# Gated experts with residual in fp32: carried pair sums closed from their PSUM banks, the second pass's x operands made during the first pass, and the last two pairs of features multiplied straight into rows

## The chip, the cores and the metric

The kernel runs on one core of a Trainium2 chip. The metric is the device time of one execution in microseconds (us). The engines are named as in the profile: PE (TensorE, with PEld for its weight loads), DVE (VectorE), ACT (ScalarE), POOL (GpSimd) and SP (SyncE, which issues nearly all DMAs here).

## The reference, cut to what matters

```python
# x: (8, 512, 256); 8 experts and one shared expert; F = 1024
g = einsum('bsd,edf->ebsf', x, Wg);  u = einsum('bsd,edf->ebsf', x, Wu)
expert_outs = einsum('ebsf,efd->ebsd', silu(g) * u, Wd)
expert_output = einsum('be,ebsd->bsd', gates, expert_outs)
shared = (silu(x @ Sg) * (x @ Su)) @ Sd
return x + (1 - sg) * expert_output + sg * shared
```

Everything is fp32. Each of the nine experts is evaluated for every token.

## The kernel before

The eight sequences are done in two passes `h` of four (NI = 4), so that a pass needs the transposed x of four sequences only. A pass goes over nine experts and two groups of four 128-wide pieces of F: 18 units in a pass, 36 in all, numbered `u.n` = 0 to 35. In one unit, four pieces `i` of the weights meet four sequences `j`, so there are 16 feature tiles h[i, j] of 128 x 512. Gate and up (`m` = 0 and 1) contract over D = 256, two halves of 128.

Plainly this would be 64 matmuls of 128 x 512 for gate and up and 32 for down. The kernel spends 52 and 26. It gives the weight pieces and sequences constants CI = (0, 1, -1, 2) and treats the six pairs in PAIRS, (1,0), (0,2), (3,0), (1,2), (3,1), (3,2), together: differences and sums of operands are prepared so that part of the products is shared.

**Gate and up** (`gate_up`). A unit has 52 steps "G". The first 16 are the hub, on the diagonal tiles: `P_step` (L370), `Q_step` (L392) and, for pair 0, `R1_step`. Then come six blocks, one for each pair, of two `R1_step` (L411) for the pair after it and four `R_step` (L421). The chain of one tile is: ACT copies a start value into a PSUM bank (L406, `seed`), PE adds a matmul (L411), DVE makes the start of the partner bank from it (L416), PE adds L421, DVE adds a kept tile where needed (L426), ACT takes silu of the gate bank (L356), and DVE multiplies gate, coefficient and up bank into h (L361). The banks `g0` and `g1` have three buffers each. DVE also makes the difference X of a pair's two features (L435). POOL adds the features up into four `rows` and four `cols` sums (L446), and prepares the weight forms (L291 to L313, L340, L345). `make_ad` (ACT, L333) makes `a2`, twice the first half of the down weights, which the forms of some pairs use.

**Down** (`down`) runs up to a unit behind, in steps "D" between the G steps, from G number 22 of its own unit to G 22 of the next. The two banks `po0` and `po1` alternate. A pair takes three matmuls: r = Wd h[i,j] (L494), S = Wd h[j,i] (L483), and a second one on top of r's bank with X (L511). Sums are carried over all 18 units of a pass in SBUF: B_j, b_j (the two halves of the output), V_p and S_p. `put` adds a bank to such a sum on DVE (L470). `carried` does it on PE: ACT copies the sum into the bank (L482), the matmul adds, ACT copies the bank out (L487). In the kernel before all six S_p are carried this way (OWN = all pairs). Then, for each i, one matmul of `rows` into b_i ("p", L483) and one of `cols` into B_i ("q", L494).

**Closing a pass.** In the last unit of each pass (u.n = 17 and 35) the sums are combined. `pair` appends to a list `combos`: V -= S, B_i -= S, b_i += V/d, b_j -= V/d; `ends_of` appends B_i -= c b_i. `combine` takes entries from the list and runs each as a DVE operation with both operands in SBUF (L557, L559). Then `turn_back` transposes every 128 x 128 block on PE (L143, `pto`), adds x (L584) and stores.

**x operands of the second pass.** In unit 17, from G 18, `turn_x` loads rows of x, transposes them on PE (`ptx`) and evicts them (L165, L169); `make_forms` makes the pair forms v, b0, b1 for pairs 0 to 2 (DVE L185 to L188, POOL L189), and unit 18 makes the other three (L205, L207, L219, L220). Forms are stored to DRAM (`xs`); each unit loads them from there (L209 for v, L226 for b).

The order on PE and POOL is the order of the program text (`manual_schedule`, HAND; in unit 0 ACT's too). The order on DVE, ACT and SP is set by a scheduler when the kernel is built. `ORDER` is the string of G and D steps of a unit: `HUB = "GGD" * 8`, then six times `"GGDGGDGGD"`.

Of the kernel before, what the change touches and what calls it, by code (L numbers as in the profile page):

```python
# [16 lines left out]
def kernel(  # L17
# [37 lines left out]
    nc = tc.nc  # L55
# [11 lines left out]
    OWN = (0, 1, 2, 3, 4, 5)  # L67
# [17 lines left out]
    iopool = ctx.enter_context(tc.tile_pool(name="io", bufs=2))  # L85
# [37 lines left out]
    made = []  # L123
    xhub = {}

# [29 lines left out]
    def turn_x(h, pool, tag, loaded=None):  # L155

        rows = loaded or [load_rows(pool, tag, NI * h)]
        for i in range(NI):
            xt = xpool.tile([P, 2, S], F32, tag="x", name=f"x{h}_{i}")
            for n_, k in enumerate((0, 1) if CI[i] == 0.0 else (1, 0)):  # L160
                pt, n = new_po(f"ptx{h}_{i}_{k}", h > 0)
                turn(pt, [rows[i][t // 2][:, t % 2, ts(k, P)] for t in range(NT)])
                turned[n] = True
                if k == 1:
                    nc.scalar.copy(xt[:, 1], pt)  # L165
                elif CI[i] == 0.0:
                    ve.tensor_copy(xt[:, 0], pt)
                else:
                    ve.scalar_tensor_tensor(  # L169
                        xt[:, 0], xt[:, 1], -CI[i], pt, ALU.mult, ALU.add  # L170
                    )
                if n_ == 1:
                    xhub[h, i] = xt
                    if len(rows) < NI:
                        rows.append(load_rows(pool, tag, NI * h + i + 1))
                yield

    def make_forms(h, p):

        i, j = PAIRS[p]  # L180
        d = CI[i] - CI[j]
        v, b0, b1 = (
            zpool.tile([P, S], F32, tag="z", name=f"f{k}{h}_{p}") for k in range(3)
        )
        ve.tensor_sub(v, xhub[h, i][:, 0], xhub[h, j][:, 0])  # L185
        if d != 1.0:
            ve.tensor_scalar(v, v, 1.0 / d, None, ALU.mult)
        ve.tensor_add(b0, v, xhub[h, j][:, 1])  # L188
        gp.tensor_tensor(b1, v, xhub[h, i][:, 1], ALU.add)  # L189
        made.append((h, p, (v, b0, b1)))  # L190

    def store_made():
        for h, p, tiles in made:
            scratch[h, p] = dram.tile([P, 3, S], F32, tag=f"xs{h}_{p}", name=f"xs{h}_{p}")
            for k, t in enumerate(tiles):
                nc.sync.dma_start(scratch[h, p][:, k], t)
        made.clear()
# [126 lines left out]
    def make_ad(u):  # L324
        a, A = u.raw_d[:, :, 0:P], u.raw_d[:, :, P : 2 * P]
        t = dpool.tile([P, NI - 1, P], F32, tag="ad", name=f"ad{u.name}")
        for i in range(NI):
            u.ad[i] = A[:, i]
            if CI[i] != 0.0:
                u.ad[i] = t[:, i - 1]  # L330
                at_of(u.ad[i], CI[i], a[:, i], A[:, i])
        u.a2 = dpool.tile([P, NI, P], F32, tag="a2", name=f"a2{u.name}", bufs=1)
        nc.scalar.mul(u.a2, a, 2.0)  # L333
# [96 lines left out]
    def h_sums(u, p):  # L430


        i, j = PAIRS[p]
        u.X[p] = tpool.tile([P, S], F32, tag="t", name=f"X{p}_{u.name}")
        ve.tensor_sub(u.X[p], u.h_[j, i], u.h_[i, j])  # L435
        for k, l in ((i, j), (j, i)):
            for which, n in (("rows", k), ("cols", l)):
                u.sums.append((which, n, (k, l)))
# [13 lines left out]
    combos = []  # L452

    def down(u, acc):
# [21 lines left out]
        def carried(key, w, b):  # L476

            po, k = new_po(f"{key[0]}{key[1]}_{u.name}")
            seeded = key in acc and not turned[k]
            turned[k] = False  # L480
            if seeded:
                nc.scalar.copy(po, acc[key])  # L482
            nc.tensor.matmul(  # L483
                po, w, b, start=not seeded, stop=True, skip_group_check=seeded
            )
            if seeded:
                nc.scalar.copy(acc[key], po)  # L487
            else:
                put(key, po, 1.0)

# [6 lines left out]
        def pair(p):  # L497
            i, j = PAIRS[p]
            d = CI[i] - CI[j]
            A, k = single(("r", p), u.Wd[p][i], u.h_[i, j])  # L500
            put(("B", j), A, 1.0)
            held[k] = True
            yield
            if p in OWN:
                carried(("S", p), u.Wd[p][j], u.h_[j, i])
            else:
                o, _ = single(("s", p), u.Wd[p][j], u.h_[j, i])
                put(("B", i), o, -1.0)
                put(("V", p), o, -1.0)
            yield  # L510
            nc.tensor.matmul(  # L511
                A, u.Ud[p], u.X[p], start=False, stop=True, skip_group_check=True
            )
            put(("V", p), A, 1.0)
            held[k] = False
            po_next[0] = 1 - k
            if u.closes:
                V, b = acc["V", p], (acc["b", i], acc["b", j])
                if p in OWN:
                    combos.append((V, -1.0, acc["S", p]))  # L520
                    combos.append((acc["B", i], -1.0, acc["S", p]))
                combos.append((b[0], 1.0 / d, V))
                combos.append((b[1], -1.0 / d, V))
            yield

        def ends_of(i):
            if CI[i] != 0.0:
                combos.append((acc["B", i], -CI[i], acc["b", i]))
            combos.append((u.h, i, acc))

        for p in range(5):
            yield from pair(p)
        for what in ("p0", "q0", 5, "q1", "p1", "q2", "p2", "q3", "p3"):
            if what == 5:
                yield from pair(5)
                continue
            i = int(what[1])
            if what[0] == "p":
                flush_sums(u, "rows", i)
                carried(("b", i), u.raw_d[:, i, 0:P], u.rows[i])  # L540
# [4 lines left out]
            if u.closes and what in ("q0", "p1", "p2", "p3"):  # L545
                ends_of(i)
            yield

    def combine():

        to, s, what = combos.pop(0)
        if not isinstance(s, float):
            h, i, acc = to, s, what
            for r in (0, 1):
                ends[h, i, r] = acc["bB"[r], i]
        elif s in (1.0, -1.0):
            ve.tensor_tensor(to, to, what, ALU.add if s > 0 else ALU.subtract)  # L557
        else:
            ve.scalar_tensor_tensor(to, what, s, to, ALU.mult, ALU.add)  # L559
# [13 lines left out]
    def turn_back(h, i, r):  # L573

        b = NI * h + i
        block = ends.pop((h, i, r))
        xr = load_back(h, i, r)
        if h + 1 < NH:
            pt, n = new_po(f"pto{b}_{r}", True)
            turned[n] = True  # L580
        else:
            pt = ps_g.tile([P, S], F32, tag=f"g{r}", name=f"pto{b}_{r}")
        turn(pt, [block[:, ts(t, P)] for t in range(NT)])
        ve.tensor_add(xr, pt.rearrange("p (t d) -> p t d", t=NT), xr)  # L584
        nc.sync.dma_start(block_of(out, b, r), xr)
        n = BACK.index((i, r)) + 1
        if h + 1 < NH and n < len(BACK):
            load_back(h, *BACK[n])

# [5 lines left out]
    def gate_up(u, nxt):  # L595
# [41 lines left out]
        for p in range(len(PAIRS)):  # L637
# [9 lines left out]
            if p == 5:  # L647
                store_made()
                if nxt is not None:
                    load_d(nxt)  # L650
# [19 lines left out]
    FIRST = "TGGTGGTGG" + "G" * 16 + BLOCK * 5  # L670

# [17 lines left out]
    turning = turn_x(0, hpool, "h", loaded)  # L689
# [8 lines left out]
    behind, acc = iter(()), {}  # L698
    for u in units:
# [6 lines left out]
        for what in ORDER if u.n else FIRST:  # L706
            if what == "G":
# [6 lines left out]
                if final and nxt is not None:  # L714
                    if nG == 18:
                        turning = turn_x(u.h + 1, iopool, "io")
                    if nG >= 18 and nG % 3 == 0:
                        next(turning, None)
                    if nG in (33, 39, 45):
                        make_forms(u.h + 1, (nG - 33) // 6)  # L720
                    if nG in (39, 45, 51):
                        store_made()
                if nG > TAKE and nG % 2 == 0 and len(u.sums) > 0:
                    add_sum(u)
# [4 lines left out]
            elif what == "T":  # L729
                for _ in range(2):  # L730
                    next(turning, None)
            else:
                next(behind, None)
                since_close += 1
                for _ in range(2 if nxt is not None else len(combos)):
                    if combos:
                        combine()
                if since_close in BACK_AT:
                    turn_back(u.h - 1, *BACK[BACK_AT.index(since_close)])
        for _ in g:  # L740
            pass
        if u.n == 0:
# [4 lines left out]
    for n, at in enumerate(BACK):  # L747
        load_back(NH - 1, *at, *((zpool, "z") if n < 6 else (iopool, "io")))
    for _ in behind:
        while combos:  # L750
            combine()
    for i, r in ((0, 0), (0, 1), (1, 0), (1, 1), (2, 0), (2, 1), (3, 0), (3, 1)):
        turn_back(NH - 1, i, r)
# [37 lines left out]
```

## Time and profile before

| | us |
|---|---|
| median of three runs | 2517.24 |
| lowest, highest | 2516.68, 2518.9 |
| the profiled execution, whole time | 2516.66 |
| its span, first to last instruction | 2514.8 |
| PE busy in the span | 2454.0 (98%) |
| POOL busy | 2080.4 (83%) |
| DVE busy | 1891.1 (75%) |
| ACT busy | 1328.8 (53%) |
| mean granted PE clock | 0.994 |

A matmul of 128 x 512 in fp32 is two instructions in the profile, so counts on PE are twice those in the code. Times in the trace are microseconds from the start of the span. An "idle before" of an engine is the time it stood still before an instruction, with what ended it. Durations in a list overlap a little[...]; so the distance between two starts is the better measure of what one costs.

### The profile page before, as it was taken

The numbers are of one execution on the slowest core, as the hardware profiler recorded it, in microseconds if no ns is written. First come the engines' busy times: TensorE is split into PE (matmuls) and PEld (weight loads), VectorE is DVE, ScalarE is ACT, GpSimd is POOL, SyncE is SP. The second block draws the span as 40 slices with busy tenths as digits, with TensorE's granted clock in tenths as the row PEclk, the third lists the DMA queues.
The fourth block names the chain that finished last, engine by engine and source line by source line (L and its number), as shares of the span: only waits on it lengthen the run. The fifth ranks groups of instructions, "written<-read, shape, count | busy, mean of one in ns | idle before, by whom it ended". The sixth has DMA issues, their size and how long they took to land.

```text
span 2514.8 us, 22640 instructions
## 1 busy us (share of the span) xinstructions
PE 2454.0 (98%) x5752; PEld 1079.7 (43%) x5752; DVE 1891.1 (75%) x2758; ACT 1328.8 (53%) x2484; POOL 2080.4 (83%) x2296
## 2 busy tenths in 40 slices
PE   7999999999999999999799999999999999999996
PEld 3444444444444444444344444444444444444442
DVE  6677777777777777777987777777777777777778
ACT  4555555555555555555345555555555555555552
POOL 6888888888888888888688888888888888888884
PEclk9999999999999999999999999999999999999999
DMA  4332333333333223333443333323333333333231
GB/s 147 96 90 84 91 100 97 100 101 101 93 100 92 91 87 94 89 96 93 142 135 99 93 89 96 93 87 89 96 96 101 101 100 98 95 94 95 84 96 42
DMA packets 180464, 242.97 MB, mean 97 GB/s; under 512 B 13296, under 2 KB 121840, under 8 KB 180336
## 3 DMA queue, kind: packets, MB, share of 16 engines
q1 hardware_dynamic: 180048, 241.49, 31.7%
q8 instruction: 48, 0.79, 0.1%
q14 instruction: 80, 0.66, 0.1%
q10 hardware_dynamic: 288, 0.04, 0.0%
HBM read 227.84 MB, written 13.63 MB: 96 GB/s over the span
## 4 chain that ended last, share of the span: by engine, by line
PE 93%; DVE 4%; issue 1%; ACT 1%; DMA 0%; POOL 0%; DVEq 0%; SPq 0%; ACTq 0%; POOLq 0%
PE c L421 28%; PE c L411 14%; PE c L392 10%; PE c L370 10%; PE r L511 7%; PE S L483 7%; PE r L494 7%; PE b L483 5%; PE q L494 5%; DVE h L361 1%; DVE accV L557 1%; DVE X L435 0%; DVE c L426 0%; DVE accB L557 0%; DVE accb L557 0%
## 5 line engine op out<-in xcount | busy, mean ns | idle before, releaser
L421 PE MATMUL c<-b,wb 128*128 128x512 f32 x1728 | 851.0, 594 | 0.0
L361 DVE SCALAR_TENSOR_TENSOR h<-sg,coef,c 128x512 f32<-128x512 f32 x576 | 428.5, 744 | 359.7 <-PE c L421 248.0
L356 ACT ACTIVATE sg<-c 128x512 f32<-128x512 f32 x576 | 344.5, 598 | 619.2 <-DVE c L426 360.4
L421 PEld LDWEIGHTS c<-b,wb 128*128 128x128 f32 x1728 | 328.2, 191 | 407.9 <-issue 385.2
L411 PE MATMUL c<-v,u 128*128 128x512 f32 x864 | 445.0, 597 | 16.4 <-ACT c L406 11.5
L446 POOL TENSOR_TENSOR rows<-rows,h 128x512 f32<-128x512 f32 x288 | 383.8, 1333 | 3.8 <-DVE h L361 3.8
L446 POOL TENSOR_TENSOR cols<-cols,h 128x512 f32<-128x512 f32 x288 | 369.6, 1283 | 0.0
L416 DVE TENSOR_TENSOR c<-D,c 128x512 f32<-128x512 f32 x432 | 299.4, 693 | 91.0 <-ACT sg L356 69.6
L312 POOL TENSOR_TENSOR wb<-u,wb 128x256 f32<-128x256 f32 x108 | 80.9, 749 | 295.4 <-ACT wb L310 295.4
L426 DVE TENSOR_TENSOR c<-c,D 128x512 f32<-128x512 f32 x432 | 299.2, 693 | 22.8 <-PE c L421 21.3
L370 PE MATMUL c<-x,w 128*128 128x512 f32 x576 | 276.7, 593 | 2.5 <-ACT sg L356 1.8
L411 PEld LDWEIGHTS c<-v,u 128*128 128x128 f32 x864 | 161.2, 190 | 233.7 <-issue 182.1
L511 PE MATMUL r<-X,ud 128*128 128x512 f32 x432 | 224.0, 600 | 11.2 <-DVE accB L470 11.2
L483 PE MATMUL S<-h,wd 128*128 128x512 f32 x432 | 222.1, 596 | 6.5 <-ACT S L482 6.4
L494 PE MATMUL r<-h,wd 128*128 128x512 f32 x432 | 221.5, 594 | 0.0
L435 DVE TENSOR_TENSOR X<-h,h 128x512 f32<-128x512 f32 x216 | 212.8, 985 | 5.9
L392 PE MATMUL c<-x,at 128*128 128x512 f32 x432 | 210.2, 595 | 1.2 <-DVE P L385 1.1
L446 POOL TENSOR_TENSOR rows<-h,h 128x512 f32<-128x512 f32 x144 | 207.2, 1439 | 0.0
L398 ACT COPY D<-c 128x512 f32<-128x512 f32 x288 | 169.1, 588 | 58.2 <-DVE h L361 58.1
L482 ACT COPY S<-accS 128x512 f32<-128x512 f32 x201 | 119.0, 592 | 140.1 <-DVE accV L470 132.1
L446 POOL TENSOR_TENSOR cols<-h,h 128x512 f32<-128x512 f32 x144 | 186.7, 1296 | 0.0
L375 ACT COPY P<-c 128x512 f32<-128x512 f32 x216 | 126.6, 587 | 101.9 <-PE c L370 97.2
(90 smaller groups left out, 3318.4 us busy)
## 6 DMA issues: line engine op xcount, KB each, us to landing
b<-xs SPq DMA_DIRECT2D x207, 512.0 KB, 3.5
v<-xs SPq DMA_DIRECT2D x207, 256.0 KB, 2.6
w<-in_L_cond_Wg_dram SPq DMA_DIRECT2D x128, 128.0 KB, 3.4
w<-in_L_cond_Wu_dram SPq DMA_DIRECT2D x128, 128.0 KB, 3.6
wd<-in_L_cond_Wd_dram SPq DMA_DIRECT2D x32, 512.0 KB, 4.9
xs<-b SPq DMA_DIRECT2D x9, 512.0 KB, 3.1
xin<-in_x_dram SPq DMA_DIRECT2D x16, 256.0 KB, 3.9
xr<-in_x_dram SPq DMA_DIRECT2D x16, 256.0 KB, 3.1
```

The lines of the kernel that those rows point to most:

```text
L356: nc.scalar.activation(s, bank, AF.Silu)
L361: ve.scalar_tensor_tensor(t, u.sg[i, j], coef[:, u.e, b : b + 1], bank, ALU.mult, ALU.mult)
L370: nc.tensor.matmul(bank, u.raw[i][:, m, 0], xhub[u.h, i][:, 0], start=True, stop=True)
L392: nc.tensor.matmul(bank, u.at[i][:, m], xhub[u.h, i][:, 1], start=False, stop=True, skip_group_check=True,)
L411: nc.tensor.matmul(bank, u.U[p][:, m], u.V[p], start=False, stop=True, skip_group_check=True)
L416: ve.tensor_sub(other, u.Ds[j, m], bank)
L421: nc.tensor.matmul(bank, u.W[p][:, r, m], u.VB[p][:, r], start=False, stop=True, skip_group_check=True,)
L426: ve.tensor_add(bank, bank, u.Ds[j, m])
L446: gp.tensor_tensor(sums[n], u.h_[n, n] if first else sums[n], u.h_[at], ALU.add)
L483: nc.tensor.matmul(po, w, b, start=not seeded, stop=True, skip_group_check=seeded)
L494: nc.tensor.matmul(po, w, b, start=True, stop=True)
L511: nc.tensor.matmul(A, u.Ud[p], u.X[p], start=False, stop=True, skip_group_check=True)
```

## The change

1. **Closing from the banks.** `combos`, `combine` and `ends_of` are gone. In the closing units S goes from its bank into B_i and V (two `put`); DVE adds the carried V into the bank of r in place, and the bank is put into b_i and b_j. What `carried` returns (the bank, where it was seeded) is put into B_i in place of the SBUF sum.
2. **OWN = (0, 1, 2, 3)**: S of pairs 4 and 5 is not carried; in every unit it is put from its bank into B_i and V.
3. **`a2`** is made by POOL in place of ACT.
4. **`prepare`** makes the x operands of the second pass in units 2 to 13, one step at every fourth D step: loads, transposes, evictions to the `io` pool (4 buffers, before 2), stores to DRAM, then for each of the six pairs four loads, three or four POOL operations and three stores. Unit 17 loads the finished x (`load_x`).
5. **The last unit** has its own order, LAST. Pairs 4 and 5 are not "starred" there: no X, no sums, no down matmuls of their own; their carried sums are closed in unit 34. Their four features h[1,3], h[3,1], h[3,2], h[2,3] are multiplied as stationary operands with the down weights (`tail`: four matmuls of 256 columns each), straight into rows of the output. x for the end is loaded as rows (two tiles of 2 KB a partition for each sequence), and stored so. The down steps of this unit are closer together, and transposes, tails and stores (B, X, S) are interleaved with the last G steps.

```diff
-    OWN = (0, 1, 2, 3, 4, 5)
+    OWN = (0, 1, 2, 3)
...
+    def prepare(h):
...
+        for i in range(NI):
+            to = xdram[h, i] = dram.tile([P, 2, S], F32, tag=f"xd{h}_{i}", name=f"xd{h}_{i}")
+            rows = load_rows(iopool, "io", NI * h + i)
...
+            for k in (1, 0):
+                pt, n = new_po(f"ptx{h}_{i}_{k}", True)
+                turned[n] = True
+                turn(pt, [rows[t // 2][:, t % 2, ts(k, P)] for t in range(NT)])
+                both[k] = tile_of(f"xt{i}_{k}_")
+                if k == 1 or CI[i] == 0.0:
+                    nc.scalar.copy(both[k], pt)
+                else:
+                    ve.scalar_tensor_tensor(both[0], both[1], -CI[i], pt, ALU.mult, ALU.add)
+                yield
...
+        for p, (i, j) in enumerate(PAIRS):
...
+            v = at[0]
+            gp.tensor_tensor(v, v, at[1], ALU.subtract)
+            if d != 1.0:
+                gp.tensor_scalar(v, v, 1.0 / d, 0.0, ALU.mult, ALU.add)
+            yield
+            gp.tensor_tensor(at[2], v, at[2], ALU.add)
+            yield
+            gp.tensor_tensor(at[3], v, at[3], ALU.add)
...
+            for k, n in ((0, 0), (1, 2), (2, 3)):
+                nc.sync.dma_start(to[:, k], at[n])
...
-        nc.scalar.mul(u.a2, a, 2.0)
+        gp.tensor_scalar(u.a2, a, 2.0, 0.0, ALU.mult, ALU.add)
...
+    def starred(u, p):
+        return u.n + 1 < len(units) or p < 4
+    def closes(u, p):
+        return u.closes and starred(u, p) or u.n + 2 == len(units) and p >= 4
...
-            if p in OWN:
-                carried(("S", p), u.Wd[p][j], u.h_[j, i])
+            args = u.Wd[p][j], u.h_[j, i]
+            if p in OWN and not closes(u, p):
+                carried(("S", p), *args)
             else:
-                o, _ = single(("s", p), u.Wd[p][j], u.h_[j, i])
+                if p in OWN:
+                    o, full = seeded(("S", p), *args)
+                    if not full:
+                        ve.tensor_add(o, o, acc["S", p])
+                else:
+                    o, _ = single(("s", p), *args)
                 put(("B", i), o, -1.0)
                 put(("V", p), o, -1.0)
...
-            put(("V", p), A, 1.0)
+            if closes(u, p):
+                ve.tensor_add(A, A, acc["V", p])
+                put(("b", i), A, 1.0 / d)
+                put(("b", j), A, -1.0 / d)
+            else:
+                put(("V", p), A, 1.0)
...
+        if u.n + 1 < len(units):
+            order = (0, 1, 2, 3, 4, "p0", "q0", 5, "q1", "p1", "q2", "p2", "q3", "p3")
+        else:
+            order = (0, 1, 2, "q0", 3, "p0", "q3", "q1", "p3", "q2", "p1", "p2")
...
+    def tail(u, i, j, first):
+        for t in range(NT):
+            bank = tails[j][t // 2][:, t % 2]
+            nc.tensor.matmul(
+                bank, u.h_[i, j][:, ts(t, P)], u.raw_d[:, i],
+                start=first and t % 2 == 0, stop=True, skip_group_check=True,
+            )
...
+    LAST = (
+        HUB + BLOCK * 4 + "GDGDGDGDGGD" + "GDGDBGDBGDGDGDS"
+        + "BBXBBXBBXXSSS"
+    )
...
-                if final and nxt is not None:
-                    if nG == 18:
-                        turning = turn_x(u.h + 1, iopool, "io")
...
+                if final and nxt is not None and nG in (18, 21, 24, 27):
+                    load_x(u.h + 1, (nG - 18) // 3)
...
+                if ahead is not None and u.n >= 2 and since_close % 4 == 0:
+                    next(ahead, None)
```

## The prediction

> **What bounds the kernel now.** I read the engines' busy time by stretches first, since shares over the whole span hide the ends (columns: window, its length, then busy us and instruction count of PE, PEld, DVE, ACT, POOL; granted clock; DMA):
>
> ```profile
> 0.00:85.00 85.00, 70.79 (x174) 30.32 (x175) 52.95 (x76) 37.76 (x70) 62.17 (x82) 0.96 0.43 143
> 85.00:1165.00 1080.00, 1079.09 (x2511) 475.48 (x2510) 804.79 (x1187) 591.46 (x1109) 913.62 (x1015) 1.00 0.31 94
> 1165.00:1325.00 160.00, 142.08 (x358) 62.98 (x357) 142.44 (x193) 68.38 (x126) 124.74 (x123) 0.96 0.40 127
> 1325.00:2440.00 1115.00, 1112.74 (x2589) 490.19 (x2588) 827.19 (x1222) 611.98 (x1146) 942.25 (x1050) 1.00 0.31 94
> 2440.00:2515.00 75.00, 49.34 (x126) 20.73 (x124) 63.76 (x81) 19.27 (x36) 37.65 (x29) 0.93 0.19 58
> ```
>
> In the two long stretches PE is full: 1080 / 2511 = 0.43 us an instruction, 0.86 a matmul. At this pace the others lose: the start has 134 full instructions and 32 transposes of 0.11 us (61 of 85 us used: 24 lost), the middle 294 and 64 (133 of 160: 27 lost), the end 94 and 32 (44 of 75: 31 lost). Some 80 us are to be had, none in between.
>
> Next, the list by line says what DVE costs (mean ns last):
>
> ```profile
> L470 DVE TENSOR_TENSOR accV<-r,accV 128x512 f32<-128x512 f32 x204 | 139.4, 683 | 0.8 <-PE r L511 0.4
> L557 DVE TENSOR_TENSOR accV<-accV,accS 128x512 f32<-128x512 f32 x12 | 16.1, 1344 | 0.0
> ```
>
> The timeline of DVE and then of PE in the last unit (start, us, operation, idle before it) shows the closing operations in a row, and PE waiting behind them:
>
> ```profile
> 2461.90 1.39 DVE L435 TENSOR_TENSOR X<-h,h 128x512 f32<-128x512 f32 x1
> 2463.22 1.75 DVE L557 TENSOR_TENSOR accV<-accV,accS 128x512 f32<-128x512 f32 x1
> 2464.89 1.75 DVE L557 TENSOR_TENSOR accB<-accB,accS 128x512 f32<-128x512 f32 x1
> 2466.56 3.42 DVE L559 SCALAR_TENSOR_TENSOR accb<-accV,accb 128x512 f32<-128x512 f32 x2
> ```
> ```profile
> 2471.24 1.12 PE L511 MATMUL r<-X,ud 128*128 128x512 f32 x2 [2.83 <-DVE accB L470]
> 2481.77 1.12 PE L511 MATMUL r<-X,ud 128*128 128x512 f32 x2 [3.37 <-DVE accB L470]
> 2491.97 2.07 PE L483 MATMUL S<-h,wd 128*128 128x512 f32 x2 [5.76 <-ACT S L482]
> ```
>
> DVE is 97% busy from 2436 to 2491 (53.15 of 55 us) and from 1191 to 1255 (61.78 of 64): it is the bound of both closings. At the start POOL and ACT hold each other up over a2:
>
> ```profile
> 33.46 0.73 POOL L345 TENSOR_TENSOR wd<-ud,a 128x256 f32<-128x256 f32 x1 [3.49 <-ACT a L333]
> ```
> ```profile
> 37.86 0.63 ACT L333 ACTIVATE a<-wd 128x512 f32<-128x512 f32 x1 [3.54 <-POOL wd L345]
> ```
>
> [...] 683 ns from a bank, 1344 from two SBUF tiles beside a busy POOL. [...] the matmul at 2491.97, behind a 5.76 us wait, took 2.07 us, others 1.02.
>
> **The change, part by part.** The base is the profiled execution: span 2514.8, 2516.66 in all, 0.6 below the median.
>
> *Start, a2.* POOL now makes a2 itself. Not in the trace; [...] 1.33 (two inputs here); I take 0.9. POOL then goes on at about 30.9 where it went on at 33.46: 2.6 earlier. ACT's seeds at 33.21 lose the 0.53 of a2 ahead of them, and its silu at 38.40 no longer queues behind the second a2. The next limit is L421 at 34.88 and the DVE/ACT chain after it, so PE's 42.09 moves by 2 to 3. I take -2.5 (bounds 0 and -5).
>
> *Steady units, DVE.* S of pairs 4 and 5: two puts each, 4 x 0.60 us a unit (starts back to back are 0.60 apart); ACT drops four copies of 0.59. Cover: in the hub after 686 DVE idles 1.95, 1.59, 0.57, 1.61 us, waiting for PE or ACT. S of pair 4 (L483 at 687.60) ends at 688.6, inside the 1.95; S of pair 5 (700.48) at 701.5, inside the 1.61. I cost it at 0; without that cover it is 2.4 us a unit.
>
> *Steady units, POOL.* a2 sits at the head of the hub, where POOL ran from 683 to 649 of the next cycle without a pause. Behind it queue the last sums; the tightest is the cols sum that ended at 641.24 for the q matmul at 643.43: 2.2 us of slack, against 0.9. Cost 0. After the hub POOL idles 3.04, 3.54, 2.04 us on ACT wb, so it recovers.
>
> *Units 2 to 13, prepare.* POOL: 6 x 3 additions and three scalings, 18 x 1.3 + 3 x 0.9 = 26 us over some 7.5 units; where two meet a2 in a hub, 0.9 + 2.6 passes the 2.2. SP: 8 row loads, 8 + 18 stores and 24 loads, in one queue with v, b and the weights. A store waits for POOL or ACT, a load for a store that frees its buffer, about 3 us (xs<-b lands in 3.1); a b load has 7.7 - 3.5 = 4.2 us to spare. So mostly hidden: I take +3 (0 to 15). The 8 transposes (0.44 us each, 3.5) move here from unit 17; one follows an S matmul on the same bank and waits for its eviction: +1 beyond the 3.5.
>
> *Middle.* Before, each closing pair took DVE 14 us (its L416 starts at 1203.33, 1217.31, 1231.80), where PE needs 9 x 0.86 = 7.7. Now a pair has 13 operations: ten at 0.60, two h at 0.65, one X at 1.0: 8.3 us. One loop comes in: the last b put frees the bank, ACT seeds it (0.6), PE runs S (1.0), DVE takes S; DVE has 1.8 us of other work for it, so I add 0.3: 8.6. Five pairs from about 1191.9 (1.3 earlier, since three transposes are gone): 9.4 + 3 x 8.6 + 7.5 + some waiting ends at 1235.5, before 1253.7: -18.2. Hub and turn-back after it, with fewer queued DVE operations: 18.5 to 17.0 us and 2.5 of PE waits and clock: -4. The 3.5 of transposes come back above: -19 net (bounds -13, -23).
>
> *Unit 34.* Pairs 4 and 5 close there: four more DVE operations on top of the four, 2.4 us more in a hub whose 5.9 us of idle they share: +0.7 (0 to 2).
>
> *End.* PE: 12 instructions of 0.43 less, 32 of half length more: +1.7 us, inside what follows. DVE from 2436.4: the pair period is as above: 2445.8, 2454.5, 2463.0; the block of pair 4 has 15 operations with a wait for S and X: 2473.8; the next ends with the last h at 2482.7. After it six operations of 0.60, [...] and 3.4 us of tails: last DVE end 2493.7. Then the last store; before, 2510.4 to 2514.8 = 4.4: end at 2498. Against 2514.8: -17 (bounds -12, -20).
>
> Sum: -2.5 + 3 + 1 - 19 + 0.7 - 17 = -33.8: 2516.7 - 33.8 = 2483.
>
> **Rivals.**
> - *The loop replaces the wait*: bank, seed, S, puts run in series, 10.5 us a pair in place of 8.6. 1.9 x 9 pairs = +17: 2500. For it: ACT S waits already follow DVE (L482 <- DVE accV, 132 us in all). Against: those stand where DVE is late anyhow.
> - *Units 2 to 13 suffer*: a b load is held behind a store once a pair cycle, 1 to 2 us in ten units: +14: 2497. For it: SP's order is fixed beforehand. Against: 4.2 us of slack.
> - *Slower*: a2 on POOL holds up every hub. Place: the q matmul of sequence 2; it decides from 2.2 us on, and undoes all at 2.2 + 34 / 36 = 3.2 us. At 4 us: 36 x 1.8 - 34 = +31: 2548. Against: two inputs take 1.33 at most on average.
> - PE full in the closings too, so that nothing comes: excluded by its 27 and 31 us of loss.
>
> **The numbers.** The sum 0.66; the loop 0.15; first pass 0.13; slow a2 0.05; about nothing 0.01. Faster by over 0.2% (5 us, about what can be told from no change): 0.93; within 0.02; slower 0.05. The range: -45 if start, middle and end reach their better bounds, so 2472; upwards it takes in the first-pass case and most of the loop's: 2499.
>
> **What will show it.** Right: no POOL wait on a2; closing pairs 8.5 to 9 us apart on DVE; PE's losses near 21, 8 and 20 us in the three stretches; units 2 to 13 at 67 us each, plus 0.9 where transposes fall; last DVE operation 4.4 us before the end. Wrong: PE waits on cols or rows sums in hubs, on v or b in units 2 to 13, ACT S seeds that wait over 1 us in each closing pair, or a store that lands later than 4.4 us.

## The result, and the profile after

| | before | after |
|---|---|---|
| median, us | 2516.96 | 2478.2 |
| lowest, highest | 2516.15, 2518.9 | 2474.26, 2479.64 |
| the profiled execution, whole time | 2516.66 | 2474.26 |
| its span | 2514.8 | 2472.4 |

The ratio is 0.9842, with a 95% interval of 0.9825 to 0.9859: 38.8 us faster. The profiled execution of after is its fastest, so the spans differ by 42.4; the runs below show which parts of that are scatter.

The five stretches of the kernel after, with the columns of before (length; busy us and count of PE, PEld, DVE, ACT, POOL; clock; DMA):

```profile
0.00:85.00 85.00, 72.46 (x182) 31.27 (x183) 57.83 (x81) 37.98 (x71) 66.11 (x86) 0.98 0.44 146
85.00:1165.00 1080.00, 1075.86 (x2529) 476.64 (x2528) 844.67 (x1252) 554.07 (x1027) 945.09 (x1045) 1.00 0.35 108
1165.00:1325.00 160.00, 154.27 (x379) 68.02 (x378) 132.40 (x197) 77.16 (x143) 129.73 (x147) 1.00 0.38 117
1325.00:2440.00 1115.00, 1112.32 (x2590) 491.28 (x2589) 879.84 (x1311) 572.94 (x1059) 959.45 (x1062) 1.00 0.32 95
2440.00:2473.00 33.00, 24.95 (x96) 14.90 (x94) 23.25 (x43) 5.21 (x9) 0.00 (x0) 1.00 0.16 64
```

The third line is the reading to make: PE has 154.27 busy of 160 us where it had 142.08. The second went the other way: 1075.86 of 1080 where it was 1079.09, the price of the work put into the first pass. The granted clock of the third stretch rose with it, from 0.96 to 1.00: before, it stood at half for 13.7 us of units 17 and 18 (a clock of 0.50 from 1220.72 to 1227.54, 1248.02 to 1251.43 and 1292.40 to 1295.81), and after for none, which is up to 6.8 us of PE's work within the gain there.

Windows at fixed times compare different work, since the kernel after is ahead. So the table below cuts each trace at the first `Q_step` matmul of a unit's hub (L392 before, L423 after), which has the same place in each unit:

| stretch | before | after | difference | predicted |
|---|---|---|---|---|
| start to the hub of unit 1 | 87.01 | 83.38 | -3.6 | -2.5 |
| units 1 to 16 | 1074.14 | 1080.03 | +5.9 | +7.5 |
| units 17 and 18 | 168.48 | 145.32 | -23.2 | -22.5 |
| units 19 to 33 | 1007.75 | 1004.25 | -3.5 | 0 |
| unit 34 | 68.09 | 66.95 | -1.1 | +0.7 |
| unit 35 to the end | 109.33 | 92.47 | -16.9 | -17 |
| span | 2514.8 | 2472.4 | -42.4 | -33.8 |

The closing of a pass on DVE: one operation of each pair (L447, before L416) and the new ones, from the timeline of DVE in unit 17 of the kernel after:

```profile
1203.72 0.68 DVE L447 TENSOR_TENSOR c<-D,c 128x512 f32<-128x512 f32 x1
...
1206.24 0.68 DVE L511 TENSOR_TENSOR accV<-accV,S 128x512 f32<-128x512 f32 x1
...
1209.36 0.69 DVE L565 TENSOR_TENSOR r<-r,accV 128x512 f32<-128x512 f32 x1
...
1211.75 0.69 DVE L447 TENSOR_TENSOR c<-D,c 128x512 f32<-128x512 f32 x1
...
1220.32 0.68 DVE L447 TENSOR_TENSOR c<-D,c 128x512 f32<-128x512 f32 x1
```

A pair takes 8.03 and 8.57 us here, where it took 14. The operations that read a bank take 0.68 us; those of L557 that they replace took 1.34 in the mean of their largest group. Reading a bank is not faster in itself: in the kernel before, the same L557 operations (four records of 0.02 us apart) took 0.68 to 0.69 us wherever POOL stood idle through them, and all but one of those that overlapped with a POOL operation took 0.79 to 1.78. The 561 puts from a bank (L470) took 0.68 to 0.69 us each, 516 of them beside a POOL operation. What the banks save is the collision with POOL.

What PE waits for (us in all, times, longest), in the kernel before and then in the kernel after:

```profile
PE r L511 <- DVE accB L470: 11.2, 4, 3.4
PE S L483 <- ACT S L482: 6.4, 2, 5.8
```

```profile
PE c L442 <- ACT c L437: 9.7, 6, 2.3
PE q L538 <- POOL cols L479: 2.3, 1, 2.3
...
PE S L522 <- ACT S L521: 1.7, 3, 0.6
...
PE r L538 <- DVE accb L513: 1.6, 1, 1.6
...
PE ptx L143 <- ACT accS L530: 1.0, 1, 1.0
...
PE c L452 <- DMA b<-xs: 0.8, 2, 0.6
```

The 11.2 us of r behind accB are gone, but for one wait of 1.6 us for accb in the last unit, and the 6.4 us of S behind its seed have become 1.7. New are three waits of the first pass: a cols sum, a transpose behind S, and b loads. The end, from the timeline of DVE:

```profile
2456.94 0.75 DVE L392 SCALAR_TENSOR_TENSOR h<-sg,coef,c 128x512 f32<-128x512 f32 x1
...
2468.59 0.69 DVE L653 TENSOR_TENSOR xin<-tail,xin 128x512 f32<-128x512 f32 x1 [0.17 <-PE tail L644]
```

The last h ends at 2457.7 and the last DVE operation at 2469.3; the last store lands 3.1 us later.

### The profile page after: what moved, and what is told of

The parts are those of the page before. It is cut to its first block, busy times and chain, and to the rows that moved or that the text cites. A ratio compares the mean times of both kernels' runs of the same rounds, so it can differ in the third digit from the quotient of the medians.

```text
span 2472.4 us, 22803 instructions
## 1 busy us (share of the span) xinstructions
PE 2439.9 (99%) x5772; PEld 1082.1 (44%) x5772; DVE 1938.0 (78%) x2880; ACT 1247.4 (50%) x2305; POOL 2100.4 (85%) x2339
## 5 line engine op out<-in xcount | busy, mean ns | idle before, releaser
L392 DVE SCALAR_TENSOR_TENSOR h<-sg,coef,c 128x512 f32<-128x512 f32 x576 | 428.1, 743 | 244.4 <-PE c L452 139.6
L479 POOL TENSOR_TENSOR rows<-rows,h 128x512 f32<-128x512 f32 x284 | 374.7, 1319 | 0.0
L447 DVE TENSOR_TENSOR c<-D,c 128x512 f32<-128x512 f32 x432 | 299.2, 692 | 85.7 <-ACT sg L387 64.2
L479 POOL TENSOR_TENSOR cols<-cols,h 128x512 f32<-128x512 f32 x284 | 362.9, 1278 | 0.0
L561 PE MATMUL r<-X,ud 128*128 128x512 f32 x428 | 218.6, 592 | 0.0
L423 PE MATMUL c<-x,at 128*128 128x512 f32 x432 | 210.0, 595 | 0.9 <-DVE P L416 0.9
L479 POOL TENSOR_TENSOR rows<-h,h 128x512 f32<-128x512 f32 x144 | 197.5, 1371 | 0.0
L401 PEld LDWEIGHTS c<-x,w 128*128 128x128 f32 x576 | 109.1, 190 | 136.4 <-issue 112.4
L521 ACT COPY S<-accS 128x512 f32<-128x512 f32 x135 | 79.7, 590 | 155.4 <-DVE accV L509 145.6
```

Of the source, the lines that this page charges most:

```text
L392: ve.scalar_tensor_tensor(t, u.sg[i, j], coef[:, u.e, b : b + 1], bank, ALU.mult, ALU.mult)
L401: nc.tensor.matmul(bank, u.raw[i][:, m, 0], xhub[u.h, i][:, 0], start=True, stop=True)
L423: nc.tensor.matmul(bank, u.at[i][:, m], xhub[u.h, i][:, 1], start=False, stop=True, skip_group_check=True,)
L447: ve.tensor_sub(other, u.Ds[j, m], bank)
L479: gp.tensor_tensor(sums[n], u.h_[n, n] if first else sums[n], u.h_[at], ALU.add)
L561: nc.tensor.matmul(A, u.Ud[p], u.X[p], start=False, stop=True, skip_group_check=True)
```

## The experiments

Each run was timed beside the kernel before. All intervals are 95% and of the ratio to the kernel before. The stretches of the profiled executions (us; cut as above) are what most verdicts rest on. A row is one profiled execution, so differences of 2 to 3 us between rows can be scatter:

| run | start | 1 to 16 | 17, 18 | 19 to 33 | 34 | 35 to end |
|---|---|---|---|---|---|---|
| before | 87.01 | 1074.14 | 168.48 | 1007.75 | 68.09 | 109.33 |
| before, a2 on POOL | 83.95 | 1071.20 | 166.99 | 1004.25 | 66.95 | 111.86 |
| before, OWN of four | 86.53 | 1074.06 | 167.90 | 1007.63 | 67.32 | 107.26 |
| before, bank closing | 85.43 | 1074.94 | 161.94 | 1007.40 | 67.59 | 102.80 |
| after | 83.38 | 1080.03 | 145.32 | 1004.25 | 66.95 | 92.47 |
| after, a2 on ACT | 88.02 | 1103.75 | 145.26 | 1007.65 | 67.12 | 92.50 |
| after, no prepare | 83.96 | 1071.20 | 161.52 | 1004.25 | 66.95 | 92.22 |
| the same, a2 on ACT | 84.30 | 1074.41 | 159.55 | 1007.94 | 67.08 | 92.42 |
| after, x prepared, forms not | 85.86 | 1076.26 | 152.78 | 1004.25 | 66.95 | 92.40 |
| after, plain last unit | 86.17 | 1081.40 | 147.00 | 1004.25 | 66.94 | 99.84 |
| after, a2 four times | 84.77 | 1097.70 | 147.81 | 1016.38 | 67.80 | 92.94 |
| after, hub free | 84.58 | 1078.62 | 147.00 | 1004.25 | 66.95 | 92.50 |
| after, again | 85.04 | 1082.87 | 145.31 | 1004.25 | 66.95 | 92.48 |
| after, both moves | 86.11 | 1075.49 | 145.34 | 1004.25 | 66.95 | 92.46 |

**The parts alone, on the kernel before.** First a2:

```diff
-        nc.scalar.mul(u.a2, a, 2.0)
+        gp.tensor_scalar(u.a2, a, 2.0, 0.0, ALU.mult, ALU.add)
```

> The kernel before with one edit: a2 made on POOL. Theory: the start loses the mutual wait of POOL and ACT, 2.5 us in the prediction, 3.6 us in the profile of after (first hub matmul 87.01 to 83.38), and nothing is paid in the 35 other hubs, where the cols sums have 2.2 us of slack and a2 takes 0.62. So -2.5 to -4 us. Rival, slow a2: POOL's hub is the later one and each hub pays; the kernel becomes slower by up to 20 us. A second rival, that a2 off ACT also explains the 3.5 us that units 19 to 33 took less in the profile of after: then -6 to -8 in all, with units 19 to 33 at 66.95 us each in place of 67.18.

Measured: 2506.39 us, 0.996 (0.9949 to 0.9971), 9.6 us less. My theory had -2.5 to -4 and was wrong; the second rival is right, and more than it said: units 1 to 18 and unit 34 gain too. Units 19 to 33 take exactly the 1004.25 of the kernel after, units 1 to 16 take 2.9 us less. The end took 2.5 us longer (111.86). But this is one profile, with a mean granted clock of 0.992 where that of before has 0.994; so the 2.5 us are not put down to a2. Where the gain sits is seen in a unit of the second pass with one of the longest waits. The kernel before, timelines of ACT and PE:

```profile
1902.16 0.63 ACT L333 ACTIVATE a<-wd 128x512 f32<-128x512 f32 x1 [1.68 <-DMA wd<-in_L_cond_Wd_dram]
1902.69 0.57 ACT L487 COPY accS<-S 128x512 f32<-128x512 f32 x1
1903.16 0.59 ACT L406 COPY c<-f 128x512 f32<-128x512 f32 x1
```
```profile
1903.85 1.10 PE L411 MATMUL c<-v,u 128*128 128x512 f32 x2 [0.64 <-issue]
```

ACT stands for 1.68 us before a2, until the down weights of the next unit have landed. Behind it in ACT's order is the copy that seeds the next bank; it ends at 1903.75, and PE's L411 starts 0.1 us later. The unit took 67.83 us in place of 66.95. With a2 on POOL the same matmul follows its forerunner without a gap, at 1893.79 behind 1892.93. The profile names the gap "issue", so the list of PE's waits doesn't name its cause; the list of ACT's waits of the kernel before does:

```profile
ACT a L333 <- DMA wd<-in_L_cond_Wd_dram: 29.8, 30, 1.7
ACT a L333 <- DMA wd<-in_L_cond_Sd_dram: 4.5, 4, 2.0
```

Then OWN:

```diff
-    OWN = (0, 1, 2, 3, 4, 5)
+    OWN = (0, 1, 2, 3)
```

> The kernel before with one edit: OWN = (0, 1, 2, 3), so that S of pairs 4 and 5 is put on DVE in every unit and is no longer carried. Theory: 0 in the steady units (the 2.4 us of DVE work a unit lie in idle time of the hub), and 4 closing operations fewer between SBUF tiles at the two closings together with 8 puts from banks, so within 2 us of the kernel before. Rival, ACT relief: it explains the 3.5 us of units 19 to 33, then these units take 66.95 us in place of 67.18 and the kernel is 5 to 8 us faster. Rival, no cover: up to 2.4 us a unit, slower by tens of us.

Measured: 2515.36 us, 0.9999 (0.999 to 1.0008). No difference: the DVE puts are covered in the steady units (1074.06 and 1007.63 against 1074.14 and 1007.75), and ACT's four copies fewer bring nothing either. The 2.1 us less from unit 35 on (107.26) stand in one profile only. What the edit buys is room: two sums of 2 KB a partition are gone, and `io` has two more buffers of that size.

Then the closing alone:

```diff
-            if p in OWN:
-                carried(("S", p), u.Wd[p][j], u.h_[j, i])
+            if p in OWN and not u.closes:
+                carried(("S", p), *args)
...
-            put(("V", p), A, 1.0)
+            if u.closes:
+                ve.tensor_add(A, A, acc["V", p])
+                put(("b", i), A, 1.0 / d)
+                put(("b", j), A, -1.0 / d)
...
-                for _ in range(2 if nxt is not None else len(combos)):
-                    if combos:
-                        combine()
```

> The kernel before with the closing from the banks alone (no x made ahead, a2 on ACT, all six S carried, the last unit's order and its turn-back as before). Theory: a closing pair takes DVE 8.6 us in place of 14 when nothing else runs there; in unit 17 the forms and the x of the second pass still lie on DVE and PE, so I expect 12 to 16 us less in the middle, and 8 to 12 us less at the end, where six pair periods shrink but the last two pairs' features still wait for their matmuls: -20 to -28 in all. Rival, the loop bank, seed, matmul, puts in series takes the place of the wait: pairs 10.5 us apart, and only -10 to -14 in all.

Measured: 2501.82 us, 0.9942 (0.993 to 0.9955), 14.2 us less; too little for my theory, and within the number of the rival. But the rival's mechanism is not it: in unit 35 the pairs stand 7.8, 9.4, 8.0 and 8.6 us apart (second L416 of each: 2420.45, 2428.25, 2437.61, 2445.63, 2454.20). Only in unit 17 are they 10.9, 11.5 and 13.5 apart. The timeline of PE there:

```profile
1197.52 0.66 PE L143 MATMUL ptx<-ident,xin 128*128 128x128 f32 x4 [1.25 <-DVE accV L470]
1203.48 0.65 PE L143 MATMUL ptx<-ident,xin 128*128 128x128 f32 x4 [1.00 <-DVE accb L470]
1208.88 0.65 PE L143 MATMUL ptx<-ident,xin 128*128 128x128 f32 x4 [1.31 <-DVE accV L470]
1215.01 0.66 PE L143 MATMUL ptx<-ident,xin 128*128 128x128 f32 x4 [1.18 <-DVE accb L470]
1221.22 1.09 PE L143 MATMUL ptx<-ident,xin 128*128 128x128 f32 x4 [2.12 <-DVE accV L470]
```

The transposes of x need a po bank, and now DVE reads the bank of S twice and that of r three times after X, where it was once, before they are free. Five waits, 6.9 us. Bank closing takes work from DVE, and the transposes take part of it back as waits.

**Undoing a2 in the kernel after.** The diff above, reversed.

> The changed kernel with one edit undone: a2 made on ACT. Theory: +2.5 to +4 us, all of it before the first hub (first hub matmul back near 87); the wait of 2.3 us for a cols sum in unit 10 is gone with it, so +1 to +4 in all. Rival: a2 on ACT slows the later units, +6 to +8, units 19 to 33 back at 67.18 us each.

Measured: 2503.87 us, 0.9953 (0.9939 to 0.9967): 25.7 us worse than the kernel after, which neither theory had. Units 19 to 33 are back at 1007.65; by far the most, 23.7 us, lies in units 1 to 16. Timelines of POOL, SP's queue, ACT and PE in unit 11:

```profile
802.52 1.27 POOL L217 TENSOR_TENSOR f<-f,f 128x512 f32<-128x512 f32 x1
```
```profile
803.81 0.32 SPq L222 DMA_DIRECT2D xs<-f  x1
804.22 2.00 SPq L206 DMA_DIRECT2D f<-xd  x2
...
808.27 0.41 SPq L350 DMA_DIRECT2D wd<-in_L_cond_Wd_dram  x1
```
```profile
814.55 0.63 ACT L364 ACTIVATE a<-wd 128x512 f32<-128x512 f32 x1 [6.30 <-DMA wd<-in_L_cond_Wd_dram]
815.09 0.57 ACT L530 COPY accS<-S 128x512 f32<-128x512 f32 x1
815.55 0.59 ACT L437 COPY c<-f 128x512 f32<-128x512 f32 x1
```
```profile
816.25 2.05 PE L442 MATMUL c<-v,u 128*128 128x512 f32 x2 [5.26 <-issue]
818.09 1.91 PE L452 MATMUL c<-b,wb 128*128 128x512 f32 x2
```

Prepare's last addition on POOL ends at 803.79; its store on SP starts at 803.81, then come prepare's next loads, and wd, behind them in the same queue, is issued at 808.27, 33.5 us into the unit (from 774.77). Without prepare it is issued 29.5 us into unit 11 (782.95 from 753.46). There it also lands sooner, 4.9 us after its issue in place of 6.2. ACT's a2 waits 6.30 us for it, the seed stands behind a2, and PE loses 5.26 us and then runs at half speed (2.05 and 1.91 us a matmul, where others take 1.02). Units 6 and 12 show the same, with waits of a2 of 4.80 and 4.37 us; these three units hold 17.8 of the 23.7 us. In the kernel after the load is as late (795.02 from 760.91, 34.1 us), and no wait for it shows on any engine.

**Prepare, and the fourth corner.** Without prepare, `turn_x` and `make_forms` are back in unit 17:

```diff
-                if final and nxt is not None and nG in (18, 21, 24, 27):
-                    load_x(u.h + 1, (nG - 18) // 3)
+                if final and nxt is not None:
+                    if nG == 18:
+                        turning = turn_x(u.h + 1, iopool, "io")
+                    if nG >= 18 and nG % 3 == 0:
+                        next(turning, None)
+                    if nG in (33, 39, 45):
+                        make_forms(u.h + 1, (nG - 33) // 6)
...
-                if ahead is not None and u.n >= 2 and since_close % 4 == 0:
-                    next(ahead, None)
```

> The changed kernel without prepare: x of the second pass is turned in unit 17 and its forms are made in units 17 and 18, as in the kernel before. Theory from the runs so far: units 1 to 16 fall from 1080.0 us to 1071.2 (the pace of the kernel before with a2 on POOL), and units 17 and 18 rise from 145.3 us to about 160 (161.9 with bank closing alone, less 1.5 for a2); net +4 to +8. Prediction's terms: prepare costs 7.5 in the first pass and is worth most of the middle. Rival: closing from banks does the middle by itself, units 17 and 18 stay near 150 and the kernel is faster without prepare by 4 us.

Measured: 2481.43 us (2480.64 to 2482.57), 0.9861 (0.9848 to 0.9875): 3.2 us more than the kernel after, whose times (up to 2479.64) lie all below it. This is less than the +4 to +8 expected, and the two intervals overlap; the stretches are the firmer evidence. They fall as expected: 1071.20, and 161.52 in the middle. So prepare costs 8.8 us in the first pass (1080.03 less 1071.20) and earns 16.2 in the middle (161.52 less 145.32); against the repeated profile of the kernel after, below, it costs 11.7 and earns the same.

> The changed kernel without prepare and with a2 on ACT: the fourth corner of prepare by a2. Theory: a2 on ACT is dear where prepare fills SP's queue, because ACT's a2 stands ahead of the seeds and waits for the wd load, which is issued late there. Without prepare units 1 to 16 take about 1074 us (1103.75 with both, 1071.2 without either), the whole about +10 against the changed kernel without prepare. Rival: a2 on ACT collides with the evictions of the new code whatever SP does, then units 1 to 16 stay near 1100.

Measured: 2490.93 us, 0.9907 (0.9892 to 0.9921); units 1 to 16 at 1074.41. As expected. The four corners, in medians: prepare with a2 on POOL 2478.2, on ACT 2503.9; no prepare with a2 on POOL 2481.4, on ACT 2490.9. With a2 on ACT prepare would lose 13 us; with a2 on POOL it gains about 3.

Half of prepare, x turned ahead but the forms made in units 17 and 18:

```diff
-        for p, (i, j) in enumerate(PAIRS):
-            d = CI[i] - CI[j]
-            to = dram.tile([P, 3, S], F32, tag=f"xs{h}_{p}", name=f"xs{h}_{p}")
...
+                if final and nxt is not None:
+                    if nG in (33, 39, 45):
+                        make_forms(u.h + 1, (nG - 33) // 6)
```

> The changed kernel with only the first half of prepare: x of the second pass is turned and stored in the first pass and loaded in unit 17, but its forms are made in units 17 and 18 as in the kernel before. It tells which half the middle gains from. Theory of the transposes: each of them takes the one free bank of po in unit 17 and waits for DVE, 5 waits of 1 to 2 us in the bank-closing run and one of 2.9 for S; without them units 17 and 18 take 147 to 151, and units 1 to 16 about 1076, so -2 to +2 in all. Theory of the forms: DVE is the bound there and the forms' 9 to 11 us of it come on top, units 17 and 18 take 154 to 158 and the kernel is slower by 4 to 8.

Measured: 2480.34 us (2479.11 to 2480.74), 0.9859 (0.9845 to 0.9872). The middle, 152.78, lies between the two theories: 8.7 us of the 16.2 come from the transposes and evictions of x, 7.5 from the forms, taken away in this order.

**The last unit.** Its order, the tails and the row stores are taken out, the closing from banks stays:

```diff
-        return u.n + 1 < len(units) or p < 4
+        return True
...
-        for what in FIRST if u.n == 0 else LAST if nxt is None else ORDER:
+        for what in FIRST if u.n == 0 else ORDER:
```

> The changed kernel with the last unit as in the kernel before (all six pairs with X, sums and down matmuls, the ordinary order, no tails, x added in column blocks), closing from banks kept. Theory: unit 35 to the end takes 102.8 us with bank closing alone (all six S carried) and 92.5 in the changed kernel; S of pairs 4 and 5 not carried saves about 2, so 100 to 102 here, +8 to +10 in all. Units 1 to 33 unchanged. Rival, the prediction's -17 comes from the bank closing and not from the new order: then +3 or less.

Measured: 2487.4 us, 0.9883 (0.9869 to 0.9896), 9.2 more; 99.84 us from unit 35 on in place of 92.47. As expected. Of the end's 16.9 us, 7.4 are the new order with tails and row stores, 6.5 the bank closing (109.33 to 102.80), and about 3 are left; OWN had 2.1 alone (109.33 to 107.26), in one profile.

**The slow-a2 rival, priced.** The a2 instruction is issued four times:

```diff
-        gp.tensor_scalar(u.a2, a, 2.0, 0.0, ALU.mult, ALU.add)
+        for _ in range(4):
+            gp.tensor_scalar(u.a2, a, 2.0, 0.0, ALU.mult, ALU.add)
```

> The changed kernel with the a2 instruction on POOL issued four times in a row, so that a2 takes POOL 2.5 us a hub in place of 0.62. It prices the slow-a2 rival. Theory: in a unit of the second pass the tightest cols sum ends 1.4 us before its q matmul starts (1460.96 against 1462.38), so 1.86 us more makes PE wait about 0.45 us in every hub: units 19 to 33 at 67.4 to 67.9 us in place of 66.95, and +12 to +25 in all. Rival: POOL catches up before the sums (its idle time after the hub), then no change.

Measured: 2509.98 us, 0.9973 (0.9962 to 0.9984), 31.8 more. PE's longest list entry, and a2 in POOL's timeline with the sum and the matmul that wait:

```profile
PE q L539 <- POOL cols L480: 23.7, 32, 3.1
```
```profile
1472.30 2.72 POOL L365 TENSOR_SCALAR a<-wd 128x512 f32<-128x512 f32 x4
```
```profile
1486.11 1.13 PE L539 MATMUL q<-cols,ad 128*128 128x512 f32 x2 [0.53 <-POOL cols L480]
```

The rival's mechanism exists, at the place named, and costs more than the +12 to +25 expected. Units 19 to 33 took 67.76 us each, 0.81 more. I had 0.45: four in a row take 2.72, 2.10 more than one and not 1.86; less the 1.42 of slack this is 0.68, and the matmul behind the wait takes 1.13 in place of 1.02. (The 0.53 us of the line count from the end of the matmul before, which overlaps by 0.16 with the next one where there is no wait.)

**A better version.** Prepare's POOL steps stay out of the hub:

```diff
-            yield
+            yield "pool"
...
-                    next(ahead, None)
+                    if not (ahead_is == "pool" and nG <= 16):
+                        ahead_is = next(ahead, None)
```

> The changed kernel with prepare's POOL steps kept out of the hub (a step that would fall in the first 16 G steps of a unit waits for the next turn behind them). Theory: the one wait of 2.3 us for a cols sum, and the half-speed matmuls behind it, go: unit 10 at 67 us in place of 69.5, -2 to -3 in all. Rival: the later steps hold the x forms' loads and stores longer and a v or b load or ACT waits elsewhere, then no gain or a loss of a few us.

Measured: 2475.76 us (2472.91 to 2476.69), 0.9836 (0.9822 to 0.9849). The intervals overlap with that of the kernel after, so the gain rests on the trace: unit 10 falls from 69.50 to 66.95. No matmul ran at half speed behind that wait in the profile of the kernel after, though the expectation has it so (the two behind it took 1.12 and 1.02 us); the wait itself, 2.28 us, is nearly all of the 2.5 us. Units 8, 9, 12 and 13, where the steps now end up, take 0.3 to 0.7 more. Then also no transpose behind a carried S while the other bank is held, and a step that was put off is made at the next D step, not four later:

```diff
-                    if not (ahead_is == "pool" and nG <= 16):
-                        ahead_is = next(ahead, None)
+                    due = True
+                wait = ahead_is == "pool" and nG <= 16 or ahead_is == "turn" and True in held and recent[0] == "S"
+                if due and not wait:
+                    ahead_is, due = next(ahead, None), False
```

> The changed kernel with prepare's POOL steps out of the hub, as in the run before, and its transposes not placed behind a carried S on the same bank. Theory: -2 to -3 for the first as measured, and -1.0 to -1.5 for the one transpose that waits 1.03 us for S to be copied out: units 1 to 16 at 1077, -3 to -4 in all. Rival: a transpose one step later waits for another bank, then as the run before.

> The changed kernel as it is, so that the variants are compared with it on the same chip: 2478 us, 0.9842 of the kernel before; units 17 and 18 between 145.3 and 147.0, start between 83.4 and 86, which shows how far profiled executions of one kernel differ.

Measured: the best version 2472.32 us (2471.41 to 2472.42), 0.9827 (0.9814 to 0.984); the kernel after, repeated, 2477.69 (2477.42 to 2479.63), 0.9851 (0.9837 to 0.9864). It is 5.4 us faster than the kernel after on the same chip, and no time of one reaches the other. Every unit from 6 to 16 takes 66.95 us, and prepare's cost in the first pass is 4.3 us (1075.49 less 1071.20), of which eight transposes are 3.5.

## Why the prediction held, and where it did not

The sum was 2483 us, in a range of 2472 to 2499; the median is 2478.2. The mechanisms named for the middle and the end are the ones at work, and one term, put at nothing, was missed.

*Middle* (-22.5 predicted; -23.2, and -21.5 to -23.2 in five other profiles with the same middle): the sum was right, since the operations left on DVE were counted rightly. Pairs fell to 8.0 to 9.4 us, for 8.6 predicted, and PE's loss to 7.3 us (160 less 347 instructions of 0.43 and 32 of 0.11), for 8. But the working put the gain to the closing operations, gave only 1.3 us to the transposes that leave, and dropped the operations of the forms from its list of 13 without a price. The runs show the shares: 6.5 us from the banks alone, 16.2 from prepare, about half of it for the transposes and evictions of x, which wait for the banks that the new closing holds. Each part is worth this only beside the other.

*The loop* did not come: S waits for its seed 0.6 us at most, in three places.

*Start* (-2.5): the mutual wait of POOL and ACT over a2 is gone. Its size stays open: the eight profiles with one a2 on POOL start unit 1 at 83.4 to 86.2, in the mean at 84.9, and the five with a2 on ACT at 84.3 to 88.0, in the mean at 86.3; that is -1.4, and part of the -3.6 is scatter. a2 itself took 0.62 us (L364, 36 times); the 0.9 of the prediction was an estimate of mine, which no trace showed, and both lie below the 2.2 us of slack.

*Steady units* (0 for a2): this term failed. I followed a2 off ACT only at the start, where the profile had a wait of POOL for it. ACT's own wait before a2, 34.3 us in 34 units, was in the list of ACT's waits; the seed stands behind it. Moving a2 takes 2.9 us from units 1 to 16 and 3.5 from units 19 to 33, and is most of the 1.1 of unit 34, where with a2 on POOL the kernel before takes 66.95 too. These 7.5 us are the larger part of what the sum missed against the profiled execution (42.4 less 33.8, 8.6 us; against the medians it missed 5.0).

*First pass* (+7.5): it came out at +8.8 against the same kernel without prepare. The listed parts are 3.5 for transposes, 1.0 for the transpose behind S, 2.3 for one cols sum and 0.8 for b loads; 1.2 are not placed. Units 2 and 5 took 67.83 us, as forecast where transposes fall, and units 8, 9, 12 and 13 66.95; units 3 and 10 (69.08 and 69.50) hold the two waits named. The kernel after repeated has 2.8 us more there, 2.5 of it in units 10 and 11. But the term held by luck: a2 had left ACT for the sake of the start, and with a2 there it is 29.3 (1103.75 less 1074.41). For that case the rival "units 2 to 13 suffer" had the right queue and the wrong victim: not a b load, but wd, with ACT behind it.

*OWN* (0) is confirmed alone; *unit 34* (+0.7) cost nothing: the unit takes 66.95 us, as its neighbours do. *Slow a2*: 0.62 against the 1.42 us left behind it; the run with four shows where it would have decided.

*End* (-17): -16.9. The last h ends 77.8 us into unit 35, predicted 77.2; the last DVE operation came 1.1 us later than predicted, the store, now of whole rows, 1.3 sooner (3.1 in place of 4.4). The time of the half operations of the end was an estimate of mine that the trace of before did not show. In the kernel after the sixteen of them (L622, 128 x 256) take 0.42 us each and start 0.33 to 0.34 us apart where they follow at once. The instructions of the tails start 0.216 us apart, half of 0.43.

## What to carry to other kernels

An instruction that waits for a load costs whatever stands behind it in its engine's order, however short it is (here one of 0.63 us, which waited 34.3 us in 34 units; moving it took 7.5 us from units 1 to 16 and 19 to 34): look in the waits of every engine, not of the bound one alone, for small waits on a DMA, and ask who is queued behind. When a closing moves work into banks, count who else needs those banks in that stretch (here five transposes, which waited 6.9 us). Judge each part of a change beside the others: here one part loses 13 us or gains 3, depending on an edit of one line elsewhere.

## What the runs showed that I had not expected

A stall of PE can cost more than its length, and not always the same. In the kernel after the wait of 2.28 us for a cols sum was followed by one matmul of 1.12 us:

```profile
713.60 1.12 PE L538 MATMUL q<-cols,ad 128*128 128x512 f32 x2 [2.28 <-POOL cols L479]
714.56 1.02 PE L442 MATMUL c<-v,u 128*128 128x512 f32 x2
```

In the repetition of the same kernel, the same wait was followed by slow ones:

```profile
715.59 1.75 PE L538 MATMUL q<-cols,ad 128*128 128x512 f32 x2 [2.30 <-POOL cols L479]
717.13 1.92 PE L442 MATMUL c<-v,u 128*128 128x512 f32 x2
718.84 1.29 PE L452 MATMUL c<-b,wb 128*128 128x512 f32 x2
```

Unit 10 took 69.50 us in the one and 71.22 in the other. Behind the 5.26 us of unit 11 with a2 on ACT, four matmuls took 6.57 us from start to start (816.25 to 822.82) in place of 3.43. In the kernel before, the prediction's lines have waits of 2.83 and 3.37 us with a matmul of 1.12 behind them, and unit 17 has one of 3.27 us with a matmul of 2.07:

```profile
1248.11 2.07 PE L511 MATMUL r<-X,ud 128*128 128x512 f32 x2 [3.27 <-DVE accB L470]
```

So the length of the wait alone does not decide.

The granted clock goes with the slow matmuls. The two profiles of unit 10 (columns as above), the repetition first:

```profile
712.60:716.00 3.40, 1.10 (x3) 0.30 (x2) 1.38 (x2) 1.90 (x4) 3.32 (x5) 0.99 0.65 218
716.00:719.40 3.40, 3.40 (x5) 1.35 (x4) 0.69 (x1) 0.00 (x0) 3.32 (x5) 0.50 0.25 90
```
```profile
709.30:712.70 3.40, 2.02 (x5) 0.57 (x3) 2.37 (x4) 2.51 (x6) 3.32 (x5) 1.00 0.44 145
712.70:716.10 3.40, 2.50 (x6) 1.25 (x7) 0.69 (x1) 0.71 (x2) 3.32 (x5) 1.00 0.52 163
```

In the repetition PE is busy for 1.10 us of the window with the wait, and the clock of the next one is 0.50. In the first profile the wait lies in two windows, busy for 2.02 and 2.50 us, and the clock is 1.00 in both. Why the clock falls behind one wait and not behind the other is not shown. From the start of the q matmul to that of the third behind it are 4.38 us (715.59 to 719.97) in place of 2.67 (713.60 to 716.27), which is the difference of the two units, 1.7 us. In the middle it is the same: in two of the profiles a transpose of the turn-back waits 1.93 and 1.92 us, and the two matmuls behind it take 3.39 us with the plain last unit and 3.56 with the hub free, where they take 1.88 behind a wait of 1.93 us with both moves. Units 17 and 18 took 147.00 us in the first two and 145.34 in the third. So a wait of about 2 us was followed by a loss of 1.7 us more, or by none, and profiles of one kernel scatter by this much.
